# A two-layer decoder on one core: convolution by taps on VectorE, down products on two banks, query transposes behind the scores

## The chip, the cores and the metric

The kernel runs on one core of a Trainium2 chip. A core has a matrix engine (TensorE, called PE in the profile), three engines for elementwise work (VectorE or DVE, ScalarE or ACT, GpSimd or POOL), an engine that mainly issues transfers (SyncE or SP) and 16 DMA engines. Data lie in SBUF (128 partitions) and in PSUM, where TensorE writes its results. Each engine works through its own instructions in order and waits on semaphores for the others. The metric is the device time of one execution in microseconds; lower is better.

## The reference

x has 4 batches of 256 tokens with 256 features, in fp32; a context of 4 x 256 x 128 feeds a state-space branch. In each of two layers three branches are added to x, each on a layernorm of x:

```python
x = x + attn0(layernorm(x))            # 8 heads of 32, window of 64, tanh softcap
x = x + mamba0(ctx, layernorm(x))      # 256 channels, 16 states
x = x + ffn0(layernorm(x))             # ternary SwiGLU, 704 inner features
x = x + attn1(layernorm(x))            # 16 heads of 128, 4 key/value heads, causal
x = x + mamba1(ctx, layernorm(x))
x = x + moe(layernorm(x))              # 32 experts of 128, top 6 by groups, one shared
```

The state-space branch (mamba) is, for each channel e:

```python
xc = inproj @ ctx                       # 256 x 128 by 128 x 256
u  = silu(causal_conv(xc, w[e, 0:4]) + bias)        # 4 taps, each channel alone
dt, B, C = softplus(dtproj @ (xproj @ u)), ...
h[t] = h[t-1] * exp(dt * A) + dt * u * B ; y = sum_n h * C + D * u
out = y * silu(layernorm(x))
```

The dense feed-forward part is `down(silu(gate(x) * gate_s) * up(x) * up_s) * down_s`. The second attention normalises queries and keys over their 128 features, applies gains, biases and a rotation, and then a causal softmax.

## The kernel before, in words

x stays in SBUF as `x` from the first transfer to the last. The text of the kernel goes through the layers in order, but the framework's planner puts the instructions of each engine into an order of its own: it goes by the place of an instruction in the text, by when it reckons the operands to be ready, and by when a buffer of the pools comes free. So a line written earlier may be issued later. The state-space scans are generators of steps (`mamba_scan`, lines 201 to 239) which the text starts among the other work, so that the scan of one layer fills the engines while attention or a feed-forward part goes on.

**State-space front** (`mamba_front`, L150 to L199, called for two halves of the batches in each layer). For each of two blocks of 128 channels (c) it takes one PSUM bank and makes the convolution on TensorE: four matmuls (L166) whose weights `taps` are the input projection times one tap each, with the context shifted by one column per tap. ScalarE applies bias and Silu from the bank to `u` (L173). Then come the x projection (L179), dt (L188, softplus L190), `du` (L193) and y's start (L196). `conv_taps` (L297 to L317) makes the weights for a layer: a diagonal of the taps on VectorE (L304), two matmuls with ones (L311) and two products with the input projection (L312). For layer 1 it is called at L590. All banks of the front come from the pool pf, which has one.

**Scan** (`state`, L212 to L221): exp on ScalarE (L215), dt·u·B on GpSimd (L217), the scan on VectorE (L218) and its product with C (L220); the sum over states is shared by TensorE (L235 with an identity) and GpSimd (L227, L237), and L239 adds what TensorE summed. `mamba_gate` multiplies with the gate (L263), transposes (L265) and adds to x (L271).

**Feed-forward part of layer 0** (L576 to L640). There are two halves hf of 512 tokens. For each of six chunks ic of the inner features: two products of two matmuls (L606), Silu on ScalarE (L614), and the product `hT` on VectorE (L617). Then two pairs of token tiles (t2) take one bank of the pool pa (one buffer) each, 12 matmuls (L630), and L638 adds the bank to x. At the end of each half the front of layer 1 for the same half is called. ScalarE needs a different table for Silu than for the scan's Exp, and loading one shows in the trace as an instruction of its own at L215 or L614.

**Second attention** (L643 on). 16 steps: 4 batches times 4 key/value groups g. `keys_values` makes the layernorm of a batch, transposes it (`ln_transposed`, L140) and makes the keys. `queries` (L710) projects 512 query columns for two token tiles (`rotate`: L673, squares L688, rotation L693, L700, L701 to `qr`), transposes each (`transposed`: four transposes L707 into a bank of ps_t, copy L708 to `qT`), and takes the root (`rsqrt`, L665, L666) to `rq`. `score` makes the scores of a step (L771, L780, L773, L789, the softmax L799 to L804), `finish` transposes the weights (L814, L822), multiplies with the values (L827, L828) and projects out (L842). The steps are staggered: queries of one step, scores of the step ahead, the finish of the one ahead of that:

```python
qT = ap.tile([P, 4, S], F32, tag="qT", name="qT", bufs=2)
rq = queries(xnT, g, qT)
queued.append((b, g, qT, rq, kT, xnT))
if len(queued) > 1:
    score()
if len(scored) > 1:
    finish()
```

The scan of layer 1 runs beside it, 19 of its 32 steps during the first 13 attention steps (`EARLY`), and the rest beside the first half of the MoE part (L974, L979, L988), which ends the kernel. PSUM has 8 banks: in the first part pools pa 1, pb 2, pc 1, psd 2, psy 1, pf 1; in attention ps_q 2, ps_s 1, ps_t 2, ps_o 1 and the scan's 2.

Of the kernel before, what the change touches and what calls it, by code (L numbers as in the profile page):

```python
# [13 lines left out]
AF = mybir.ActivationFunctionType  # L14
# [3 lines left out]
P = 128  # L18
# [23 lines left out]
def decoder_kernel(  # L42
# [107 lines left out]
    def mamba_front(l, bp, pool):  # L150

        taps, xproj, dtproj = mw[l]
        o = l * M_COLS
        u = front.tile([P, 2, 512], F32, tag="u", name="u")
        dt = front.tile([P, 2, 512], F32, tag=f"dt{bp}", name="dt")
        du = front.tile([P, 2, 512], F32, tag=f"du{bp}", name="du")
        y = front.tile([P, 2, 512], F32, tag=f"y{bp}", name="y")
        xdbl = front.tile([40, 512], F32, tag="xdbl", name="xdbl")
        negA = front.tile([P, 32], F32, tag="negA", name="negA", bufs=2)

        bc = dpool.tile([32, 512], F32, name=f"bc{l}{bp}")

        for c in range(2):
            pi = ps(pool)
            for k in range(4):
                mm(  # L166
                    pi.rearrange("p (b t) -> p b t", b=2),
                    lhsT=taps[:, k, c * P : (c + 1) * P],
                    rhs=ctxT[:, 2 * bp : 2 * bp + 2, k : k + S],
                    start=(k == 0),  # L170
                    stop=(k == 3),
                )
            nc.scalar.activation(  # L173
                u[:, c, :], pi, AF.Silu, bias=par[:, o + M_CONVB + c : o + M_CONVB + c + 1]
            )

        px = ps(pool)
        for c in range(2):
            mm(px[0:40, :], lhsT=xproj[:, c, :], rhs=u[:, c, :], start=(c == 0), stop=(c == 1))  # L179
        nc.scalar.copy(xdbl, px[0:40, :])  # L180
        nc.sync.dma_start(out=bc, in_=xdbl[8:40, :])


        nc.scalar.activation(negA, par[:, o + M_ALOG : o + M_ALOG + 32], AF.Exp)
        nc.vector.tensor_scalar(negA, negA, 1e-25, -1.0, ALU.max, ALU.mult)
        for c in range(2):
            pd = ps(pool)
            mm(pd, lhsT=dtproj[:, c * P : (c + 1) * P], rhs=xdbl[0:8, :], start=True, stop=True)  # L188
            z = dt[:, c, :]
            nc.scalar.activation(  # L190
                z, pd, AF.Softplus, bias=par[:, o + M_DTB + c : o + M_DTB + c + 1]
            )
            nc.vector.tensor_mul(du[:, c, :], z, u[:, c, :])  # L193

            nc.gpsimd.memset(z.rearrange("p (s t) -> p s t", s=2)[:, :, 0:1], 1e28)
            nc.scalar.activation(  # L196
                y[:, c, :], u[:, c, :], AF.Copy, scale=par[:, o + M_D + c : o + M_D + c + 1]
            )
        y_of[l, bp] = y  # L199
        return dt, du, y, negA, bc  # L200
# [376 lines left out]
    with ExitStack() as ph:  # L577
# [9 lines left out]
        nc.sync.dma_start(out=dw, in_=down_in)  # L587
        nc.gpsimd.tensor_mul(dw, dw, downs.unsqueeze(1).to_broadcast([P, NIC, HID]))

        conv_taps(1)  # L590
        scans = []
        for hf in range(2):
            szs = [gates_of(2 * hf + bb, fp, 4) for bb in range(2)]
            if hf == 1:
                states(99)
            xnT = wp.tile([P, 2, 512], F32, tag="f_xnT", name="f_xnT")
            for bb in range(2):
                mamba_gate(0, 2 * hf + bb, pc, szs[bb])
                ln_transposed(2 * hf + bb, xnT[:, :, bb * S : (bb + 1) * S], pc)
            hT = wp.tile([P, NIC, 512], F32, tag="hT", name="hT")  # L600
            for ic in range(NIC):
                m = min(P, INTER - ic * P)
                pg, pu = ps(pb), ps(pb)
                for dst, w in ((pg, gw), (pu, uw)):
                    for f in range(2):
                        mm(  # L606
                            dst[0:m, :],
                            lhsT=w[:, f, ic * P : ic * P + m],
                            rhs=xnT[:, f, :],
                            start=(f == 0),  # L610
                            stop=(f == 1),
                        )
                sg = fp.tile([P, 512], F32, tag="sg", name="sg")
                nc.scalar.activation(  # L614
                    sg[0:m, :], pg[0:m, :], AF.Silu, scale=par[0:m, P_GATES + ic : P_GATES + ic + 1]
                )
                nc.vector.scalar_tensor_tensor(  # L617
                    hT[0:m, ic, :],
                    pu[0:m, :],
                    par[0:m, P_UPS + ic : P_UPS + ic + 1],  # L620
                    sg[0:m, :],
                    ALU.mult,
                    ALU.mult,
                )
            for t2 in range(2):
                pd = ps(pa)
                for t in range(2):
                    for ic in range(NIC):
                        m = min(P, INTER - ic * P)
                        mm(  # L630
                            pd[:, t * HID : (t + 1) * HID],
                            lhsT=hT[0:m, ic, (2 * t2 + t) * P : (2 * t2 + t + 1) * P],
                            rhs=dw[0:m, ic, :],
                            start=(ic == 0),
                            stop=(ic == NIC - 1),
                        )
                xb = x[:, 4 * hf + 2 * t2 : 4 * hf + 2 * t2 + 2, :]
                nc.vector.tensor_add(xb, xb, pd.rearrange("p (t d) -> p t d", t=2))  # L638
            scans.append(mamba_front(1, hf, pf))
# [4 lines left out]
    with ExitStack() as ph:  # L644
# [62 lines left out]
                nc.tensor.transpose(pt[:, i * P : (i + 1) * P], qr[:, i, :], ident)  # L707
            nc.scalar.copy(dst[:, :, c * P : (c + 1) * P], pt.rearrange("p (h t) -> p h t", h=4))  # L708

        def queries(xnT, g, qT):  # L710

            ss = small.tile([P, 2, 4], F32, tag="qss", name="qss")
            for c in range(2):
                transposed(rotate(xnT, c, g, ss[:, c, :]), c, qT)
            return rsqrt(ss, qks)

        def keys_values(b):
            xnT = work.tile([P, 2, S], F32, tag="xnT", name="xnT")
# [320 lines left out]
        for b in range(B):  # L1039
            xnT, kT = keys_values(b)  # L1040
            for g in range(NKV1):
                qT = ap.tile([P, 4, S], F32, tag="qT", name="qT", bufs=2)
                rq = queries(xnT, g, qT)
                queued.append((b, g, qT, rq, kT, xnT))
                if len(queued) > 1:
                    score()
                if len(scored) > 1:
                    finish()
                step = 4 * b + g

                with tc.issue_after(pace[-3]) if len(pace) > 2 else nullcontext():
                    if step < 13:
                        run(states, EARLY * (step + 1) // 13 - EARLY * step // 13)
                if step == 12:
                    for bb in range(2):
                        mamba_gate(1, bb, ps_t)

                    spare[:] = [psd, ps_s, psd]
                if step > 12:
                    next(moes[0])  # L1060
# [126 lines left out]
```

## Time and profile before

| what | value |
| --- | --- |
| three runs | 898.40, 910.52, 914.03 us (median 910.52) |
| the profiled execution | 899.79 us, its span 898.0 us |
| mean granted TensorE clock | 0.947 |
| second attention, 310 to 651 us | TensorE 300.7 busy of 341 |
| MoE alone, 760 to 898 us | TensorE 133.3 busy of 138 |
| scan of one state on VectorE, L218 | 1.217 us |
| product with C, L220 | 0.680 us |
| loading a table on ScalarE | 1.28 us |

The profile is of one execution. Its page gives the busy time of each engine, the span in 40 slices, and the chain of work that ended last, followed back from the end; the groups of instructions give the line, the engine, the operation, what is written from what, the count, the busy time, the mean of one in ns, and the idle time just before them with what ended it. The view of stages gives the busy time in chosen stretches. A tile named `ps` is a PSUM bank. An fp32 matmul leaves two records in the trace, a transpose of 128x128 too.

### The profile page before, as it was taken

The page shows a single profiled execution, that of the slowest core. Times are in us where ns is not written, and L with a number is a line of the kernel's source. Part 1 is how long each engine was busy: PE and PEld are TensorE (multiplying, and loading weights), DVE is VectorE, ACT ScalarE, POOL GpSimd, SP SyncE. Part 2 cuts the span into 40 slices and gives each one's busy share as a digit, 9 for nine tenths or more (in the row PEclk, how much of TensorE's full clock was granted, in tenths as well). Part 3 has the DMA queues.
Part 4 walks back from the last instruction along what each step waited for, and adds up shares of the span by engine and source line. Part 5 has one row for each costly group of instructions (what it writes and reads, how often), then busy time and mean ns, then how long its engine had stood idle before and what let it go on. Part 6 is the DMA issues. An engine that isn't in the chain of part 4 may idle for free.

```text
span 898.0 us, 10284 instructions
## 1 busy us (share of the span) xinstructions
PE 806.3 (90%) x3074; PEld 501.4 (56%) x3074; DVE 588.0 (65%) x1106; ACT 474.5 (53%) x1182; POOL 423.5 (47%) x427
## 2 busy tenths in 40 slices
PE   4888999978989887889788978997999999999997
PEld 1445656523444444647555755665666656666665
DVE  4799988985855588797769686787057676212121
ACT  2767544587949556657857754776333433211111
POOL 5456676976645527766547471422257751000000
PEclk9999767978998999999899989997999999999999
DMA  5347564583512401101112010000147753445442
GB/s 162 117 133 252 174 187 157 186 275 100 198 64 68 143 1 36 59 33 39 36 36 72 23 47 1 24 3 24 27 152 226 231 152 104 148 149 162 156 144 82
DMA packets 60999, 98.36 MB, mean 110 GB/s; under 512 B 6336, under 2 KB 26704, under 8 KB 60688
## 3 DMA queue, kind: packets, MB, share of 16 engines
q1 hardware_dynamic: 59232, 95.77, 33.6%
q10 hardware_dynamic: 1712, 1.94, 0.7%
q8 instruction: 24, 0.39, 0.2%
q14 instruction: 31, 0.25, 0.1%
HBM read 96.24 MB, written 1.44 MB: 109 GB/s over the span
## 4 chain that ended last, share of the span: by engine, by line
PE 51%; DVE 20%; ACT 10%; issue 5%; POOL 4%; DMA 1%; DVEq 0%; POOLq 0%; SPq 0%; ACTq 0%
PE ps L974 13%; PE ps L988 12%; PE ps L842 5%; DVE h L218 4%; PE ps L673 3%; DVE hc L220 2%; PE ps L606 2%; PE ps L630 2%; PE ps L827 2%; DVE ps L700 2%; ACT sc L799 2%; DVE qs L693 2%; PE ps L780 1%; ACT L215 1%; PE ps L235 1%
## 5 line engine op out<-in xcount | busy, mean ns | idle before, releaser
L217 POOL TENSOR_TENSOR db<-bt,du 128x512 f32<-128x512 f32 x128 | 162.4, 1280 | 90.7 <-DVE h L218 76.3
L218 DVE TENSOR_TENSOR_SCAN h<-h,db 128x512 f32<-128x512 f32 x128 | 152.9, 1217 | 25.9 <-ACT h L215 25.7
L974 PE MATMUL ps<-moe_xnT,w 128*128 128x512 f32 x272 | 129.0, 597 | 0.0
L988 PE MATMUL ps<-w,hT 128*128 128x256 f32 x544 | 128.7, 380 | 0.0
L979 DVE SCALAR_TENSOR_TENSOR hT<-ps,gr 128x512 f32<-128x512 f32 x64 | 44.1, 689 | 127.0 <-PE ps L974 127.0
L988 PEld LDWEIGHTS ps<-w,hT 128*128 128x128 f32 x544 | 103.2, 191 | 40.2 <-issue 29.4
L215 ACT ACTIVATE h<-dt,negA 128x512 f32<-128x512 f32 x128 | 86.2, 689 | 56.3 <-DVE hc L220 55.7
L980 ACT ACTIVATE hT<-hT 128x512 f32<-128x512 f32 x68 | 42.8, 629 | 133.8 <-DVE hT L979 133.6
L673 PE MATMUL ps<-wqkv,xnT 128*128 128x512 f32 x192 | 93.2, 597 | 8.0 <-DVE rq L665 5.6
L220 DVE TENSOR_TENSOR hc<-h,ct 128x512 f32<-128x512 f32 x128 | 85.1, 680 | 4.0 <-DMA ct<-bc 2.5
L227 POOL TENSOR_TENSOR y<-y,hc 128x512 f32<-128x512 f32 x64 | 80.8, 1274 | 7.1 <-DVE hc L220 7.1
L666 POOL TENSOR_TENSOR rq<-rq,nhalf 128x8 f32<-128x8 f32 x20 | 33.0, 1648 | 88.2 <-DVE rq L665 88.0
L974 PEld LDWEIGHTS ps<-moe_xnT,w 128*128 128x128 f32 x272 | 51.7, 191 | 36.5 <-issue 33.2
L688 ACT ACTIVATE sq<-ps 128x128 f32<-128x128 f32 x160 | 42.4, 282 | 46.2 <-PE ps L673 46.2
L799 ACT ACTIVATE sc<-sc,nm 128x256 f32<-128x256 f32 (+1 forms) x128 | 56.7, 449 | 12.2 <-DVE nm L794 8.0
L804 POOL TENSOR_TENSOR sc<-sc,rsum 128x512 f32<-128x512 f32 (+1 forms) x32 | 46.3, 1468 | 35.2 <-DVE rsum L802 33.6
L842 PE MATMUL ps<-wo,oT 128*128 128x256 f32 x256 | 57.0, 381 | 0.4 <-ACT oT L835 0.4
L842 PEld LDWEIGHTS ps<-wo,oT 128*128 128x128 f32 x256 | 48.1, 190 | 9.2 <-ACT oT L835 2.6
L673 PEld LDWEIGHTS ps<-wqkv,xnT 128*128 128x128 f32 x192 | 32.9, 190 | 29.1 <-issue 17.9
L235 PE MATMUL ps<-hc,ident 128*128 128x512 f32 x64 | 40.6, 723 | 8.1 <-DVE hc L220 8.1
L707 PE MATMUL ps<-ident,qr 128*128 128x128 f32 x160 | 28.7, 297 | 19.2 <-DVE qr L701 17.3
L237 POOL TENSOR_TENSOR y<-y,hc 128x512 f32<-128x512 f32 x32 | 40.8, 1275 | 10.4 <-DVE hc L220 5.3
(201 smaller groups left out, 1447.3 us busy)
## 6 DMA issues: line engine op xcount, KB each, us to landing
bt<-bc SPq DMA_DIRECT2D x96, 256.0 KB, 3.6
ct<-bc SPq DMA_DIRECT2D x96, 256.0 KB, 3.7
w<-in_w_dram SPq DMA_DIRECT2D x64, 256.0 KB, 3.4
gr<-gt SPq DMA_DIRECT2D x64, 256.0 KB, 3.5
wqkv<-in_wqkv_dram SPq DMA_DIRECT2D x1, 3072.0 KB, 14.4
wo<-in_wo_dram SPq DMA_DIRECT2D x1, 2048.0 KB, 8.9
x<-in_x_dram SPq DMA_DIRECT2D x4, 256.0 KB, 5.6
w<-in_ws_dram SPq DMA_DIRECT2D x4, 256.0 KB, 3.4
```

The source lines that it names most:

```text
L215: nc.scalar.activation(h, dt[:, c, :], AF.Exp, scale=negA[:, a : a + 1])
L217: nc.gpsimd.tensor_mul(db, bt, du[:, c, :])
L218: nc.vector.tensor_tensor_scan(h, h, db, 0.0, ALU.mult, ALU.add)
L220: nc.vector.tensor_mul(hc, h, ct)
L227: nc.gpsimd.tensor_add(y[:, c, :], y[:, c, :], state(n, c, bt, ct))
L235: mm(yp, lhsT=ident, rhs=hc, start=(n == 0), stop=(n == 14))
L673: mm(pq, lhsT=xnT[:, f, c * P : (c + 1) * P], rhs=wqkv1[:, f, ch * 512 : (ch + 1) * 512], start=(f == 0), stop=(f == 1),)
L799: nc.scalar.activation(part, part, AF.Exp, bias=nm[:, qc, j : j + 1], accum_out=rsum[:, qc, j : j + 1])
L804: nc.gpsimd.tensor_mul(part, part, rsum[:, qc, :].unsqueeze(2).to_broadcast([P, 4, w]))
L842: mm(pout[:, c * 256 : (c + 1) * 256], lhsT=oTs[h // 4][:, h % 4, c * P : (c + 1) * P], rhs=wo1[:, 8 * gp + h, :], start=(h == 0), stop=(h ...
L974: mm(ph_, lhsT=w[:, f * P : (f + 1) * P], rhs=xnT[:, f, :], start=(f == 0), stop=(f == 1))
L988: mm(po[t // 2][:, (t % 2) * 256 : (t % 2 + 1) * 256], lhsT=h[:, t * P : (t + 1) * P], rhs=w[:, 256:512], start=start and t % 2 == 0, stop ...
```

## The change

Three parts. In `mamba_front` for layer 1 the convolution is one matmul with the unscaled input projection per block of channels, and then four instructions on VectorE that read the bank: one product with the last tap (written to `u`), and three fused multiply-adds on 255, 254 and 253 of each batch's 256 columns, shifted by one, two and three. ScalarE then applies bias and Silu in place on `u`. The call of `conv_taps` for layer 1 goes. In the feed-forward part the two pairs of token tiles take their banks from the pools pa and pc in turn. In the second attention `queries` returns the rotated queries, and their transposes come in the text after the scores of the step ahead, which no longer wait for the new step to be queued. Layer 0 keeps its convolution on TensorE.

```diff
@@ mamba_front
         for c in range(2):
             pi = ps(pool)
+            if l == 1:
+
+                mm(
+                    pi.rearrange("p (b t) -> p b t", b=2),
+                    lhsT=taps[:, c * P : (c + 1) * P],
+                    rhs=ctxT[:, 2 * bp : 2 * bp + 2, 3 : S + 3],
+                    start=True,
+                    stop=True,
+                )
+                w = par[:, o + M_CONVW + 4 * c : o + M_CONVW + 4 * c + 4]
+                uc = u[:, c, :].rearrange("p (b t) -> p b t", b=2)
+                pt = pi.rearrange("p (b t) -> p b t", b=2)
+                nc.vector.tensor_scalar(uc, pt, w[:, 3:4], None, ALU.mult)
+                for k in range(1, 4):
+                    nc.vector.scalar_tensor_tensor(
+                        uc[:, :, k:S], pt[:, :, 0 : S - k], w[:, 3 - k : 4 - k], uc[:, :, k:S], ALU.mult, ALU.add
+                    )
+                nc.scalar.activation(
+                    u[:, c, :], u[:, c, :], AF.Silu, bias=par[:, o + M_CONVB + c : o + M_CONVB + c + 1]
+                )
+                continue
             for k in range(4):
                 mm(
@@ feed-forward part of layer 0
-        conv_taps(1)
         scans = []
...
             for t2 in range(2):
-                pd = ps(pa)
+                pd = ps((pa, pc)[t2])
@@ second attention
-        def queries(xnT, g, qT):
+        def queries(xnT, g):
 
             ss = small.tile([P, 2, 4], F32, tag="qss", name="qss")
-            for c in range(2):
-                transposed(rotate(xnT, c, g, ss[:, c, :]), c, qT)
-            return rsqrt(ss, qks)
+            qrs = [rotate(xnT, c, g, ss[:, c, :]) for c in range(2)]
+            return qrs, rsqrt(ss, qks)
...
             for g in range(NKV1):
+                qrs, rq = queries(xnT, g)
+                if queued:
+                    score()
                 qT = ap.tile([P, 4, S], F32, tag="qT", name="qT", bufs=2)
-                rq = queries(xnT, g, qT)
+                for c in range(2):
+                    transposed(qrs[c], c, qT)
                 queued.append((b, g, qT, rq, kT, xnT))
-                if len(queued) > 1:
-                    score()
                 if len(scored) > 1:
                     finish()
```

## The prediction

> **What bounds the kernel now.** I read the busy table first, then the chain, then a table of stages.
>
> Page, parts 1 and 4:
>
> ```profile
> PE 806.3 (90%) x3074; PEld 501.4 (56%) x3074; DVE 588.0 (65%) x1106; ACT 474.5 (53%) x1182; POOL 423.5 (47%) x427
> ...
> PE 51%; DVE 20%; ACT 10%; issue 5%; POOL 4%; DMA 1%; DVEq 0%; POOLq 0%; SPq 0%; ACTq 0%
> ```
>
> TensorE is busy 90% of the span, but only 51% of the chain is TensorE: there are stretches where something else ends last. The stage table tells which (columns: PE, PEld, DVE, ACT, POOL busy us with instruction counts, granted clock, DMA share, GB/s):
>
> ```profile
> 150.00:213.00 63.00, 52.92 (x194) 27.92 (x190) 51.31 (x83) 40.87 (x67) 47.53 (x51) 0.85 0.61 197
> 213.00:250.00 37.00, 35.89 (x90) 16.57 (x91) 27.17 (x34) 32.49 (x39) 25.95 (x25) 0.95 0.51 171
> 250.00:270.00 20.00, 15.70 (x53) 7.64 (x51) 9.78 (x29) 9.45 (x14) 7.71 (x16) 0.95 0.18 58
> 270.00:310.00 40.00, 36.44 (x102) 18.11 (x102) 21.62 (x30) 30.35 (x35) 22.71 (x26) 0.94 0.37 118
> 310.00:651.00 341.00, 300.74 (x1265) 199.39 (x1266) 251.60 (x524) 215.89 (x770) 166.31 (x140) 0.96 0.09 30
> 651.00:760.00 109.00, 106.59 (x381) 69.76 (x380) 72.83 (x146) 39.86 (x63) 59.94 (x57) 0.98 0.55 171
> ```
>
> The rows are: end of the layer-0 scan; FFN half 0; the passage between halves; FFN half 1; second attention; MoE beside the last scan. The change works in the first five. TensorE idles 10 us in the first, 1 in half 0, 4 in the passage, 4 in half 1 and 40 in attention; VectorE idles 12, 10, 10, 18 and 89. From 651 on TensorE has 2 us to spare in 109, and its order there is the same in the changed program: that stage keeps its length.
>
> **The change part by part.** Durations are of the profiled execution: span 898.0 us, device time 899.79. The order of instructions per engine is read from the built program, which has no times. Two records make one fp32 matmul.
>
> *Convolution by taps.* TensorE drops 16 matmuls L166 for 4, and the two matmuls L311 that made the weights. On average an L166 record is 630 ns busy, but records overlap: two 512-column records in a row take 0.86 us (L166 on the chain at 229.14). So 12 x 0.86 = 10.3 and 2 x 0.86 = 1.7: 12 us less on TensorE. VectorE drops the diagonal (L304, 1.6 at most) and two L312 of 0.68 (2.9 in all) and gains 16 taps. No tap is in the trace; the nearest rows, both reading a PSUM bank of 128x512, are
>
> ```profile
> L617 DVE SCALAR_TENSOR_TENSOR hT<-ps,par,sg 128x512 f32<-128x512 f32 (+1 forms) x6 | 4.5, 743 | 0.0
> L979 DVE SCALAR_TENSOR_TENSOR hT<-ps,gr 128x512 f32<-128x512 f32 x64 | 44.1, 689 | 127.0 <-PE ps L974 127.0
> ```
>
> I take 0.69, the row with 64 samples: 11.0 us, so +8 net on VectorE (bounds per tap 0.60, as back-to-back spacing shows elsewhere, to 0.75: +7 to +9). The Silu (0.69, L173) stays, one table load fewer among them.
>
> What lies on the path, in three places. (1) Before half 0 (150–213): TensorE stands on the chain at 203.95 with L166 for 1.81, and ACT with L173's table loads at 178.70 and 183.83, 1.28 each. The order puts 8 taps here (5.5) for 2.9 removed: +2.6 on VectorE, whose 12 us of idle time is nearly all waits on the scan's exponentials (10.0 us, L218 waiting for L215); that idle time is the cover. I take −1.8 and one table load, −1.2: **−3**. If the idle time lies at other moments than the taps, the 2.6 shows and the −1.2 is lost: ends −7 (all of TensorE's relief counts) and +3.
>
> (2) Half 0 and the passage. The other 8 taps come between the first four hT products; 10 us of VectorE idle time covers 5.5. But they push scan work back: five scan states stand behind the last hT instead of three, 2 x (1.22 for L218 + 0.68 for L220) = +3.8. The end of that scan is what half 1 needs (y, gate L263, transposes L265, x, layernorm). Against it, L166 and the wait for u leave the passage: TensorE waited 1.52 for u at 260.59, −1.5, and −0.8 is left over from the earlier L166 pairs. **+1.5**, ends −4 (the whole L166/L179 stretch, 256.3 to 263.2, leaves the path) and +5.5 (all eight taps show).
>
> *Down products on two banks*, half 1:
>
> ```profile
> 298.30 3.68 PE L630 MATMUL ps<-dw,hT 64*128 64x256 f32 x14 [0.45 <-DVE hT L617]
> 303.74 6.03 PE L630 MATMUL ps<-dw,hT 128*128 128x256 f32 x24 [1.76 <-DVE x L638]
> 310.60 1.95 PE L673 MATMUL ps<-wqkv,xnT 128*128 128x512 f32 x4 [0.83 <-issue]
> ```
>
> The second pair of token tiles waits until L638 has emptied the one bank: 1.76 us idle, and all its 24 records lie behind the last hT. With two banks both pairs run along with the hT products, and 28 records are left behind the last: 28 x 0.253 (6.03/24 and 3.68/14) = 7.1 instead of 3.68 + 1.76 + 6.03 = 11.5: −4.4. Bringing forward the others makes TensorE 3.43 + 0.86 = 4.29 us per chunk where ACT's alternation of Silu and Exp (sg at 280.76, 284.77, 288.77, 292.77) has 4.0: +0.3 for each of four, +1.2; the last two chunks run without an Exp between, one table load pair of 2.56 less, of which I count 0.6. The bank that is borrowed, pc, also serves the layernorm transposes of the first attention batch: these ran inside half 1 (275.96) and now wait for the second L638 (0.69), then copy, then L673: +1.4 beyond the 0.8 gap shown. If that cover stays, 0. Half 0 has no such wait at the moment, its four L235 fill the gap. Sum −4.4 + 1.2 − 0.6 + 1.4 = −2.4; I add −1.2, since TensorE idles 4 us in this row and the earlier matmuls fill part of it: **−3.6**, ends −6 and 0.
>
> *Query transposes behind the scores.* The waits of TensorE in 310–651 (instruction, releaser, us, times, longest):
>
> ```profile
> PE ps L707 <- DVE qr L701: 17.3, 9, 4.7
> PE ps L673 <- DVE rq L665: 5.6, 4, 1.8
> PE ps L780 <- DVE sc L773: 2.6, 3, 1.3
> PE ps L814 <- POOL sc L804: 2.1, 2, 1.5
> PE ps L737 <- ACT kT L708: 1.9, 2, 0.9
> ```
>
> 17.3 us of waiting for rotated queries is the obvious prize, and four waits make 14.3 of it (2.94 at 357.67, 3.21 at 438.90, 3.43 at 523.13, 4.72 at 611.30). But the order in which the program is issued is the planner's, not the text's: around three of the four, in batches 0, 2 and 3, L707 already stands right behind the score matmuls L771 and still does. At 438.90 all eight transposes now stand together behind L771, and more scan steps (1.9 each) get in front of the rotation on VectorE. Elsewhere scores do pass the transposes: the five short waits, 3.0 us in all, have work in front of them now. What is late next is the query itself: qT ready later, its scores at the next step later, but there a whole step (21 us) lies between. No instruction is added; SP's and POOL's orders are the same. I take **−2** (ends −17, every qr wait gone, and +6, one of the four places doubled plus a wait of 1.3 for sc in each following batch).
>
> Sum: −3 + 1.5 − 3.6 − 2 = **−7.1**: 892.7 on the profiled execution's footing.
>
> A rule that speaks against taking work from TensorE: rows first. In 150–213 the granted clock was 0.85, TensorE was busy 84%, and one pair of L235 took 2.08 us at 198.83 against 1.11 at 224.16. The Trainium skill ("TensorE: Matmul & The Clock Gate", Part 1: The HAM clock gate) says that the clock falls to half after an idle window of some 3.4 us and returns after as long a busy one. By it, thinning TensorE by 10 us in this stage could make several matmuls like that L235, at 1 us each, eating place (1)'s gain. No run here shows it yet.
>
> **Rivals.**
> A. *The qr waits go.* For it: it is the largest wait of the stage, and a transposes-last order gives the chain sq, qs, ps, qr (1.15 + 0.69 + 0.70 + 0.69 = 3.2 us) eight score matmuls to hide behind. Against it: the order at three of four places. −14 to −17 in place of −2: about −20, 880 on the profile's footing, 890 on the median's.
> B. *The change does not do what it says*: the planner holds the waits where they were, and the taps push the scans as far as TensorE is relieved: stage one 0, passage +3.8, half 1 −3.6, attention 0: 0 ± 3, 900 to 910.
> C. *Slower: the taps stand in the scan.* The pool pf has one bank. It used to be free after matmul and Silu; now it is held until the fourth tap, and taps stand among scans on an in-order VectorE. If two scan states get between the taps of each c, that is 4 x 0.69 + 2 x 1.9 = 6.6 us a bank, and TensorE waits at the next matmul on pf with everything behind it. Price: two banks before half 0, one effective, +6.6; passage +5.5; half 1 −3.6; attention 0: +8.5, 908 to 919. It decides once VectorE's idle time in 150–270 (32 us) does not lie where the taps stand. For it: VectorE is 81% busy in the first stage. Against: taps are placed among hT products that it did without idle.
>
> **How the numbers follow.** The executions shown lie at 898.4, 899.8 (profiled), 910.5 and 914.0, and 2% (18 us) is about what a measurement of this kernel can tell from no change. The profiled one is 10.7 below the median of the runs, so −7.1 gives 892.7 on its footing and 903.4 on the median's; I name 900, nearer the latter. Forecast 0.50, A 0.17, B 0.20, C 0.13. The low end is A on the profile's footing with its end of −19: 881; the high end C on the median's: 919. What passes 2% faster is A, with a little of the forecast; slower, a third of C: 0.18, 0.77, 0.05.
>
> **What would show it.** TensorE busy about 12 us lower; L166 replaced by 8 records; 16 taps near 0.69; no idle time for L638 in front of L630; hT6 to the first L673 about 4 us shorter; MoE's stretch equally long. L707 waiting for qr: 14 or more says forecast, under 5 says A. VectorE idle in 150–270 under 20 with half 1 starting 5 later says C. I am wrong if the taps take over 0.9, or if attention gets a new wait as long as those it lost.

## The result

The changed kernel takes 918.40 us (median of 4 runs, 912.06 to 921.70); the kernel before took 906.38 us beside it (median of 4, 898.40 to 914.03). The ratio is 1.0138 with an interval of 1.0091 to 1.0186: 1.4% **slower**, 12 us. The forecast was 900, six below the kernel before as measured here. The time lies in the range of 881 to 919, on the wrong side of the kernel before.

The profiled execution of the changed kernel took 912.06 us, its span 910.2. Page, part 1, busy time of each engine:

```profile
PE 797.5 (88%) x3046; PEld 497.3 (55%) x3046; DVE 598.9 (66%) x1119; ACT 471.8 (52%) x1180; POOL 421.8 (46%) x427
```

TensorE is 8.8 us less busy (806.3 before) and VectorE 10.9 more (588.0), while the span is 12.2 longer. The work moved the way that was forecast (12 less and 8 more); the time went the other way. The table of stages, with the same columns as before:

```profile
150.00:213.00 63.00, 41.02 (x166) 23.09 (x165) 52.96 (x85) 37.75 (x63) 45.91 (x47) 0.79 0.63 200
213.00:250.00 37.00, 35.38 (x86) 15.83 (x86) 26.80 (x34) 33.23 (x38) 20.76 (x23) 0.91 0.36 117
250.00:270.00 20.00, 14.89 (x47) 7.24 (x46) 15.47 (x26) 10.66 (x14) 11.93 (x12) 0.96 0.50 157
310.00:651.00 341.00, 299.55 (x1249) 196.57 (x1248) 256.77 (x530) 211.39 (x764) 167.63 (x144) 0.96 0.11 36
```

In the first row, whose length is fixed, TensorE has 11.9 us less work (52.9 to 41.0); the granted clock is 0.79, where it was 0.85. That its work was not what this stretch waited for shows in the next table: the way to half 0 became longer, not shorter.

To see where the 12 us arose, I mark six instructions that both kernels have: the second of the four additions of layer-0 attention to x (on VectorE), the addition of the first gate, the first L606 of half 0, the last addition to y of the layer-0 scan (L239), the first L606 of half 1, the first L673 of the second attention, and the end. Lines are those of the kernel before; the changed kernel's lie 19 to 21 higher.

| stretch, us | before | after | difference | forecast |
| --- | --- | --- | --- | --- |
| up to the second addition to x | 134.4 | 135.1 | +0.6 | 0 |
| to the first gate's addition | 60.3 | 58.3 | −2.0 | |
| to half 0 | 19.0 | 24.0 | +5.0 | −3 with the line above |
| half 0 to half 1 | 56.5 | 64.5 | +8.0 | +1.5 |
| (of that, to the scan's end) | 39.5 | 47.4 | +7.9 | |
| half 1 to the second attention | 40.3 | 37.1 | −3.2 | −3.6 |
| second attention to the end | 587.4 | 591.2 | +3.8 | −2 |

Two of the terms held: half 1, and the MoE part, whose stretch from the last output projection of attention to the end is 246.9 us before and 245.9 after. The 12 us arise in three places: the stretch that ends at the start of half 0, the one up to the end of the layer-0 scan, and attention.

### The profile page after: what moved, and what is told of

It is laid out like the page before. It is cut to its first block, busy times and chain, and to the rows that moved or that the text cites. A ratio compares the mean times of both kernels' runs of the same rounds, so it can differ in the third digit from the quotient of the medians.

```text
span 910.2 us, 10230 instructions
## 1 busy us (share of the span) xinstructions
PE 797.5 (88%) x3046; PEld 497.3 (55%) x3046; DVE 598.9 (66%) x1119; ACT 471.8 (52%) x1180; POOL 421.8 (46%) x427
## 4 chain that ended last, share of the span: by engine, by line
PE 41%; DVE 14%; ACT 6%; issue 2%; POOL 2%; DVEq 0%; ACTq 0%; POOLq 0%
PE ps L993 12%; PE ps L1007 12%; PE ps L861 5%; PE ps L693 3%; ACT sc L818 3%; DVE h L239 3%; PE ps L799 2%; PE ps L846 1%; DVE qs L713 1%; DVE sc L808 1%; DVE ps L720 1%; ACT sq L708 1%; PE ps L727 1%; DVE qr L721 1%; DVE nm L814 1%
## 5 line engine op out<-in xcount | busy, mean ns | idle before, releaser
L239 DVE TENSOR_TENSOR_SCAN h<-h,db 128x512 f32<-128x512 f32 x128 | 152.6, 1215 | 7.9 <-ACT h L236 6.5
L693 PE MATMUL ps<-wqkv,xnT 128*128 128x512 f32 x192 | 96.2, 614 | 7.7 <-DVE rq L685 2.5
L818 ACT ACTIVATE sc<-sc,nm 128x256 f32<-128x256 f32 (+1 forms) x128 | 56.6, 445 | 16.1 <-DVE nm L813 9.9
L693 PEld LDWEIGHTS ps<-wqkv,xnT 128*128 128x128 f32 x192 | 33.4, 195 | 29.8 <-issue 18.4
L727 PE MATMUL ps<-ident,qr 128*128 128x128 f32 x160 | 28.9, 302 | 17.6 <-DVE qr L721 13.8
```

The costliest lines, as they stand in the source:

```text
L239: nc.vector.tensor_tensor_scan(h, h, db, 0.0, ALU.mult, ALU.add)
L693: mm(pq, lhsT=xnT[:, f, c * P : (c + 1) * P], rhs=wqkv1[:, f, ch * 512 : (ch + 1) * 512], start=(f == 0), stop=(f == 1),)
L818: nc.scalar.activation(part, part, AF.Exp, bias=nm[:, qc, j : j + 1], accum_out=rsum[:, qc, j : j + 1])
```

## The experiments

One thing has to be known to read them. The first 134 us differ between executions of one and the same program: two of the kernels below (two banks; second bank only in half 0) have the instructions of the kernel before up to half 0. The second addition to x comes at 134.4 us in the kernel before and at 144.8 and 145.2 in these, with a granted clock from 75 to 100 us of 0.90, 0.69 and 0.70. So executions of one kernel spread over 12 to 15 us (the kernel before, in its three longer series), and I read the experiments twice: by the ratio over all runs, and by the lengths of the stretches after that point, which are steadier (the stretch from the first gate to half 0 is 18.9 to 19.1 in all six executions that share its program; the whole way from the second addition to half 0 is 79.3 to 81.2). Each stretch is that of one profiled execution.

**The three parts one at a time, and two together.**

The convolution alone:

```diff
 # kernel before
+            if l == 1:
+                (one matmul, four taps on VectorE, Silu in place)
-        conv_taps(1)
```

> The kernel before with the convolution by taps alone. Theory T (the taps cost the time): the loss before FFN half 1 is the convolution's, so half 0 starts 3 to 4 us later than before and half 1 a further 6 to 8 later; in all 9 to 14 us slower than the kernel before, as much as or more than the whole change. Rival R (the borrowed bank costs it, by changing the order at the end of half 0): 0 to 4 slower. Rival S (each part is harmless, together they collide): within 3 us of the kernel before.

Measured: 922.95 us, ratio 1.021 (1.0179 to 1.0242). Half 0 starts 86.2 us after the second addition (79.3 before), half 0 to half 1 takes 62.5 (+6.0), half 1 39.7. Theory T is right on the place of the loss; its size passed the range. All of its four executions lay within 0.7 us and at a low granted clock (0.914 to 0.915; the kernel before in the same series 0.932 to 0.948), and the profiled one had lost 8 us before the second addition; counted from there it is 14.5 us longer than the kernel before.

Two banks alone:

```diff
-                pd = ps(pa)
+                pd = ps((pa, pc)[t2])
```

> The kernel before with the down products on two banks alone. Theory T: the wait of 1.76 us in half 1 goes, half 1 is 3 us shorter, the passage between the halves is as long as before: 2 to 4 us faster. Rival R: the passage grows by 4 to 8 us, 2 to 6 us slower in all. Rival S: 2 to 4 faster.

Measured: 909.08 us, ratio 1.0059 (1.0023 to 1.0096). Theory T falls here: half 1 became 2.7 us shorter (37.6), but half 0 to half 1 became 6.3 us longer (62.8). Rival R is right.

The moved transposes alone (`queries` returns the rotated queries, `score()` comes ahead of `transposed`, as in the change):

> The kernel before with the query transposes behind the scores alone. Theory T: three of the four long waits keep their place, so attention (310 to 651 us before) changes by less than 3 us either way. Rival Q (the 3.8 us that the first attention batch lost come from this part): 2 to 5 us slower, and the loss lies in the first batch. The forecast's own case A (the waits go): 14 us faster.

Measured: 910.87 us, ratio 1.0042 (1.0002 to 1.0083). From the second attention to the end 589.8 us, 2.4 longer. The waits did not go. From the first L673 to the last output projection attention takes 343.9 us for 340.5, a little past theory T's 3. Rival Q is wrong on the place: up to the end of the first output projection 2.4 us are lost, but kernels without this part lose 1.7 to 3.0 there too. Where it does cost, the section on attention below shows.

Banks and transposes, without the convolution:

> The changed kernel with the convolution undone. Theory T: FFN as in the kernel with two banks, attention as in the kernel with moved transposes: 1 to 5 us faster than the kernel before, 10 to 16 faster than the changed kernel. Rival R: slower than before by 2 to 6. Rival S: 2 to 6 faster than before.

Measured: 908.13 us, ratio 1.0029 (0.9983 to 1.0076); half 0 to half 1 62.9, half 1 37.6, attention to the end 588.0. Theory T's 1 to 5 us faster than the kernel before did not come, since it still counted on the banks. As with the banks alone, the stretch before half 1 is 6.3 longer. So two parts lose in the same stretch, each about 6 us alone and 8 together: their losses overlap.

**Which half the second bank costs in.** It was given to one half only:

```diff
-                pd = ps(pa)
+                pd = ps((pa, pc)[t2 * hf])          # only half 1
+                pd = ps((pa, pc)[t2 * (1 - hf)])    # only half 0, the other kernel
```

> The kernel before, with the second bank only in FFN half 1; half 0 keeps one bank. Theory K: in half 0 the second bank lets 28 down-product records stand in one row on TensorE ahead of the last state sums (L235), which delays the end of the layer-0 scan by 6 to 7 us; in half 1 no sum stands behind and 2.7 us are won. So the passage is as before, half 1 2 to 3.5 us shorter: 1 to 4 us faster than the kernel before. Rival W (the waits of the scan's own buffers cost it, wherever the bank is): same as with two banks in both halves, 2 to 6 slower.

> The kernel before, with the second bank only in FFN half 0. Theory K: the stretch from the start of half 0 to the start of half 1 is 5 to 7 us longer (62 to 63), half 1 as before (40): 4 to 8 us slower than the kernel before. Rival W (the two halves only cost together): within 2 us.

Measured, only half 1: **902.82 us, ratio 0.9945 (0.9904 to 0.9986)**, faster than the kernel before; half 0 to half 1 57.5, half 1 37.5 (−2.8). Only half 0: 909.55, ratio 1.0027 (0.9985 to 1.0069); half 0 to half 1 62.8 (+6.3), half 1 40.1. Theory K's stretches are right in both; the total of the second was forecast as 4 to 8 slower, and its interval ends at 6. In the profiled execution with the bank in half 1 only 0.4 us of the gain are left from the second addition to the end, since 1.0 is lost ahead of half 1 and 1.4 behind it: that this kernel is faster rests on the ratio, whose interval ends just under 1.

Why half 0 loses shows in TensorE's timeline. The kernel before, end of half 0 (start, length, instruction, count of records, idle time before):

```profile
244.76 3.68 PE L630 MATMUL ps<-dw,hT 64*128 64x256 f32 x14 [0.26 <-DVE hT L617]
248.37 1.98 PE L235 MATMUL ps<-hc,ident 128*128 128x512 f32 x4
250.19 5.93 PE L630 MATMUL ps<-dw,hT 128*128 128x256 f32 x24
256.05 0.44 PE L265 MATMUL ps<-ident,yg 128*128 128x128 f32 x2
```

The same place with two banks alone:

```profile
257.83 1.02 PE L235 MATMUL ps<-hc,ident 128*128 128x512 f32 x2
258.78 7.09 PE L630 MATMUL ps<-dw,hT 64*128 64x256 f32 x28
265.80 3.90 PE L235 MATMUL ps<-hc,ident 128*128 128x512 f32 x8
269.53 0.38 PE L265 MATMUL ps<-ident,yg 128*128 128x128 f32 x2
```

Before, the second group of products could not start until L638 had emptied the bank, and the last sums over scan states (L235) got in between. With the second bank nothing holds the products back: 28 records stand in one row, and the sums behind them. The scan waits for these sums, because each frees a buffer `hc` and the last one frees y. The wait that the change removed was the gap in which the work ran on which half 1 depends.

To test this reading, the rest of the layer-0 scan was written ahead of the down products, with two banks, with one, and in the whole changed kernel:

```diff
-            if hf == 1:
-                states(99)
...
+            if hf == 0:
+                states(99)
             for t2 in range(2):
```

> The kernel before with two banks in both halves, and the rest of the layer-0 scan written ahead of the down products of half 0, not behind them; on TensorE all state sums now stand ahead of the last 40 records of the down products. Theory K (the row of 28 ahead of the sums is what cost 6 us): the scan's end comes at 40 us after the start of half 0 or earlier (46.4 with two banks), the stretch from half 0 to half 1 falls from 62.8 to 58 or less. Rival W (the sums' place does not matter, the second bank costs through the order on VectorE and GpSimd): it stays above 61.

> The kernel before with the same move of the scan's rest alone, one bank. Theory K: the sums already stood ahead of the second group before, so the move gains little: the stretch from half 0 to half 1 is 54 to 58 (56.5 before). Rival W: as much gain as with two banks, some 5 us.

> The whole changed kernel with the scan's rest written ahead of the down products of half 0. Theory K with T: the stretch from half 0 to half 1 falls from 64.5 to 57 to 60, the taps' share in it stays; the stretch before half 0 stays 2 to 6 longer than before: 4 to 7 us faster than the changed kernel, 5 to 8 slower than the kernel before. Rival (the taps' delay is the same delay and goes too): as fast as the kernel before.

With two banks the row now stands behind the sums:

```profile
247.88 1.13 PE L235 MATMUL ps<-hc,ident 128*128 128x512 f32 x2
248.85 0.59 PE L630 MATMUL ps<-dw,hT 128*128 128x256 f32 x2
249.69 1.12 PE L235 MATMUL ps<-hc,ident 128*128 128x512 f32 x2 [0.25 <-DVE hc L220]
250.66 10.17 PE L630 MATMUL ps<-dw,hT 128*128 128x256 f32 x40
```

The scan ends 34.0 us after the start of half 0 (46.4 with two banks), and half 0 to half 1 takes 54.6 us in place of 62.8. Rival W falls; with one bank the same move leaves this stretch at 57.6. But the times are 908.77, ratio 1.0033 (0.9981 to 1.0086), and 903.81, ratio 0.9999 (0.9943 to 1.0055): from the second attention to the end the first takes 601.0 us, 13.6 longer than the kernel before. The move changed half 1 as well: the products there no longer run along with the hT products, and the layer-1 fronts stand later. GpSimd is 186.0 us busy in the first 340 us of attention, where it was 166.3:

```profile
311.05:651.05 340.00, 291.45 (x1214) 192.20 (x1213) 266.13 (x538) 220.76 (x777) 186.01 (x156) 0.95 0.14 44
```

The kernel before, same length from its own first L673:

```profile
310.60:650.60 340.00, 300.33 (x1263) 199.01 (x1264) 251.03 (x523) 215.89 (x770) 166.31 (x140) 0.96 0.09 30
```

So layer-1 scan work that had run inside the feed-forward part now runs in attention, and what the shorter FFN won is given back there. In the whole changed kernel the move gives 912.33 us, ratio 1.0071 (1.0031 to 1.0112): half 0 to half 1 56.6, so the taps' share of that stretch goes with the row's; the stretch before half 0 stays long (24.3 from the first gate), and attention to the end takes 597.8, 6.6 more than in the changed kernel.

**Where the taps cost.** One front at a time, with the weights for the other one made as before:

```diff
+            if l == 1 and bp == 0:     # the front ahead of half 0; the other kernel: bp == 1
+                (taps on VectorE, lhsT=inproj1)
+        inproj1 = mw[1][0]
         conv_taps(1)
```

> The kernel before, with the convolution by taps only for the first front of layer 1, the one that runs ahead of FFN half 0; the weights for the second front are made as before. Theory T: the taps stand between the layernorm of the first batch and the start of half 0 on VectorE: 4 to 6 us slower from the first gate's addition to half 0; the rest as before. In all 3 to 7 us slower. Rival U (only the second front's taps cost): within 2 us.

> The kernel before, with the convolution by taps only for the second front, whose taps stand among the hT products of half 0. Theory T: 8 taps of 0.69 us push the scan's states back, its end comes 5 to 7 us later after the start of half 0, half 1 starts as much later: 4 to 8 us slower. Rival U: the whole loss of the convolution, 12 to 17.

Measured: first front 907.25, ratio 1.0016 (0.9971 to 1.0061); second front 910.14, ratio 1.0025 (0.9989 to 1.0060). Both expectations on the mechanism missed. With the first front's taps the stretch ahead of half 0 did not grow (16.8 from the first gate, 79.0 from the second addition); half 0 to half 1 grew by 3.4, since scan states slid into half 0. With the second front's, half 0 to half 1 took 63.1 (+6.6, as long as forecast), but the scan's end was nearly on time (40.4 after the start of half 0, 39.5 before): the delay arose behind it. By the ratios the two cost 4 us together, far below the 17 of the convolution alone; counted from the second addition in the profiled executions they are 2.5 and 7.1 us longer than the kernel before, the convolution alone 14.5.

What these two had in common was that the making of the tap weights stayed in the program. It was left in for both fronts, with nothing reading the weights:

```diff
+            if l == 1:
+                (taps on VectorE, lhsT=inproj1)
+        inproj1 = mw[1][0]
         conv_taps(1)
```

> The convolution by taps for both fronts alone, with the making of the tap weights of layer 1 (the diagonal, two matmuls and two products) left in the program, though nothing reads them. The convolution alone cost 17 us, its two fronts one at a time, which keep this work, some 1 and 4. Theory G (leaving out this early work moves the phase in which the clock is granted in layer-0 attention): the granted clock between 75 and 100 us is back at 0.85 or more, 3 to 9 us slower than before. Rival H (the two fronts together simply cost more): 14 or more slower.

Measured: 908.99 us, ratio 1.0028 (0.9987 to 1.0070). Rival H falls: with 3 us of VectorE and two matmuls more to do, it is 14 us faster than the kernel without them. Of the difference, 7.2 us lie between the second addition and half 0 (79.0 against 86.2) and 6.5 ahead of it. Not all of the loss is gone: half 0 to half 1 takes 64.8 in it, 8.3 more than in the kernel before, and from the second addition to the end its profiled execution is 7.5 us longer. The clock from 75 to 100 us was 0.86 in its profile and 0.66 in that of the convolution alone, as theory G has it. But that this is caused by the missing work was not shown: the changed kernel and the one with the bank in half 1 only (below) have the same program as the convolution alone up to half 0, and had 0.88 and 0.86 there (the second lost 8.6 us ahead of the second addition all the same, with a clock of 0.50 from 120 to 140 us). One program draws either. The part in the stretch before half 0 is another matter: it is the order, and the next experiment takes it up.

In the changed kernel, VectorE ahead of half 0:

```profile
195.15 0.40 DVE L120 BATCH_NORM_STATS2 ln_st<-x 128x6 f32<-128x256 f32 x1
...
196.46 3.03 DVE L284 TENSOR_TENSOR yg<-y,sz 128x256 f32<-128x256 f32 x1
199.41 0.17 DVE L121 BATCH_NORM_AGGREGATE ln_mv<-ln_st 128x2 f32<-128x6 f32 x1
```

GpSimd at the same time:

```profile
195.79 3.42 POOL L609 TENSOR_TENSOR dw<-dw,downs 128x1536 f32<-128x1536 f32 x1 [4.17 <-DMA dw<-in_down_dram]
199.16 1.45 POOL L258 TENSOR_TENSOR y<-y,hc 128x512 f32<-128x512 f32 x1
200.69 0.22 POOL L124 TENSOR_SCALAR ln_nb<-ln_mv 128x2 f32<-128x2 f32 x1
```

And TensorE:

```profile
204.06 1.18 PE L140 MATMUL ps<-ident,xn 128*128 128x128 f32 x4 [10.68 <-ACT xn L136]
```

A gate product that has a median of 0.42 us over its 16 instructions takes 3.03, and ends 0.3 us after GpSimd's multiplication of the down weights; the layernorm's last step stands behind it, then GpSimd's part of the layernorm, and TensorE waits 10.68 us. In the kernel before the multiplication ran from 200.57 to 204.00, behind GpSimd's part of this layernorm (197.02 to 198.60) and where VectorE was waiting for L190 anyway. In the changed kernel the transfer of dw is issued 3.1 us earlier (187.1 for 190.2) and the multiplication starts 4.8 earlier. That alone does not make the collision: with the weights' work kept, the multiplication starts 1.5 us after the first gate's addition (2.4 in the changed kernel), but the gate product stands right behind that addition, ahead of the multiplication, and takes 1.18. In the changed kernel a scan state, its product with C and a part of the layernorm stand between. With the multiplication cut into six:

```diff
-        nc.gpsimd.tensor_mul(dw, dw, downs.unsqueeze(1).to_broadcast([P, NIC, HID]))
+        for ic in range(NIC):
+            nc.gpsimd.tensor_mul(dw[:, ic, :], dw[:, ic, :], downs)
```

> The changed kernel, with GpSimd's one multiplication of the down weights (3.42 us, 128x1536) cut into six of a sixth each. In the changed kernel it runs while VectorE wants to do a gate product of 0.4 us, which takes 3.03 us there, and the layernorm of the first batch waits behind it. Theory L (the two engines exclude each other for the whole instruction): the gate product takes 1.2 us at most, the stretch from the first gate's addition to half 0 falls from 24.0 by 2 to 3 us, in all 2 to 4 us faster than the changed kernel, 8 to 11 slower than the kernel before. Rival O (the order of the taps alone makes this stretch): it stays at 24, in all 12 slower than before.

Measured: 914.55 us, ratio 1.0092 (1.0047 to 1.0138); the gate product takes 1.43, a little over the 1.2 expected, and the first gate to half 0 takes 21.4 in place of 24.0 to 25.7 in the executions with one multiplication. Theory L is right for the stretch. That leaves 2.4 us over the 19.0 before, whose cause was not tested: in the changed kernel the two dt products of the first front (L209) stand right ahead of half 0 and wait 1.20 and 1.56 us, where before (L188) they were done by 202.9. And counted from the second addition, the way to half 0 is 83.1 here and 81.1 to 86.2 with one multiplication, so the gain shows only behind the first gate. Its profiled execution, 926.59 us, is its longest (half 0 to half 1 69.3), so its later stretches are not read; the totals' intervals overlap, and the gain of 4 us against the changed kernel is not shown by them.

Last, two kernels that move or remove a part. The convolution by taps alone, with each front held back until the last addition of its FFN half:

```diff
+                last = nc.vector.tensor_add(xb, xb, pd.rearrange("p (t d) -> p t d", t=2)).ins
+            with tc.issue_after(last):
+                scans.append(mamba_front(1, hf, pf))
```

> The convolution by taps alone, each front of layer 1 held until the last addition of its own FFN half has been issued, so that no tap stands ahead of the layer-0 scan. The first scan states of layer 1 lose their place in half 1 with it and move into attention. Theory T (place of the taps, not their amount): half 0 starts as early as in the kernel before or earlier, the scan's end no later: 0 to 8 us faster than the kernel before. Rival V (11 us of VectorE work cost what they cost wherever they stand, and the scan states moved into attention lengthen it): 8 or more slower than before.

Measured: 940.14 us, ratio 1.0316 (1.0217 to 1.0414). No tap stood ahead of half 0 now, and yet half 0 started 84.0 us after the second addition, 4.7 later than in the kernel before. The scan's end came early (35.8 after the start of half 0), but half 0 to half 1 took 61.2, since the taps now stood in the passage, and attention to the end 608.6, 21 us more. Rival V is right, through the scan states that moved.

The changed kernel with the second bank only in half 1:

> The changed kernel, with the second bank only in FFN half 1. Theory K with T: the delay by the row of 28 and that by the taps lie on the same scan's end and overlap; without the row the stretch from half 0 to half 1 falls from 64.5 to 61 to 63, half 1 stays at 37 to 38: 2 to 4 us faster than the changed kernel, 8 to 11 slower than before. Rival (they add up): 58 to 59 and 6 us faster than the changed kernel.

Measured: 916.15 us, ratio 1.0094 (1.0052 to 1.0137); half 0 to half 1 63.3, half 1 37.0. The row's and the taps' delays overlap: taking one away in the presence of the other wins 1.2 us in the stretch, where alone it was worth 6.

## Why the prediction was wrong, step by step

**What bounds the kernel.** The reading "TensorE idles 10 us in the first, 1 in half 0, 4 in the passage" was right as a count and wrong in its use. I valued TensorE's relief there as time; the stretches up to half 1 end with a chain through VectorE, GpSimd and ScalarE, on which a shorter TensorE only waits longer (10.68 us at the first L140 ahead of half 0).

**(1) Before half 0**, forecast −3, measured +3.0 (−2.0 and +5.0). The failed step is "I take −1.8 and one table load, −1.2": neither was won. Two readings under it were wrong: of VectorE's 12 us of waiting only 2.1 are L218 waiting for L215 (9.6 more lie in half 0), and the diagonal ran at 18.3 us, so that of the 2.9 removed only the two L312, 1.4, leave this stretch. Still, it was not the cover that failed: with the weights' work kept, the second addition to half 0 takes 79.0 us with the first front's taps, 79.0 with both (79.3 before), and 84.0 without that work and with no tap there. What I counted as won, leaving out the weights' work, changed the order. Not on the list was GpSimd's dw product, 3.42 us, which now stood ahead of the layernorm of the first batch and blocked a gate product; it is 2.6 of the 5.0 by the split kernel, and the rest stays open.

**(2) Half 0 and the passage**, forecast +1.5, measured +8.0. I counted five scan states behind the last hT in place of three, as the trace has it, and priced them at +3.8, but put them down to the taps alone. The convolution alone brings 6.0, the banks alone 6.3, which I had at nothing. The sentence that failed is "Half 0 has no such wait at the moment, its four L235 fill the gap": the gap was how L235 came in time. The −1.5 for the wait for u and −0.8 for L166 were no gain either: from the scan's end to half 1 it takes 17.0 us before and 17.1 after. That passage is a chain (gate, transposes, x, layernorm, transposes, for one batch and then the other), and what TensorE dropped beside it did not shorten it.

**(3) Half 1**, forecast −3.6, measured −3.2. The 28 records behind the last hT took 7.09 us in the kernel with the bank in half 1 (7.1 forecast). From the last product to the first L673 the changed kernel needs 2.65 us, 1.8 more than before (+1.4 forecast):

```profile
308.25 8.15 PE L650 MATMUL ps<-dw,hT 128*128 128x256 f32 x32
317.18 0.44 PE L679 MATMUL ps<-ident,bt 128*128 128x128 f32 x2 [0.78 <-DVE x L658]
317.45 0.60 PE L140 MATMUL ps<-ident,xn 128*128 128x128 f32 x4
319.05 5.40 PE L693 MATMUL ps<-wqkv,xnT 128*128 128x512 f32 x8 [1.00 <-ACT xnT L143]
```

**(4) Attention**, forecast −2, measured +3.8. TensorE's waits from 310 to 665 us of the changed kernel (instruction, releaser, us, times, longest):

```profile
PE ps L727 <- DVE qr L721: 13.8, 8, 4.7
PE ps L799 <- DVE sc L792: 3.1, 3, 1.7
PE ps L727 <- DVE qr L745: 2.7, 3, 1.8
PE ps L693 <- DVE rq L685: 2.5, 2, 1.3
PE ps L846 <- ACT pTa L844: 2.4, 4, 1.0
PE ps L790 <- DVE e L765: 2.4, 2, 1.2
```

Most of the long waits stayed, as forecast (13.8 of 17.3, a hair under the 14 that I had named as the sign), so rival A fell for the reason given, the order. I had the wrong ones, though: 3.14, 3.94 and 4.71 us are left, and gone is the 3.43 of batch 2 (523.13), one of those that were to stay. The 3.5 us won came back as waits for the offsets, the keys and the weights; the waits of this view add up to 39 us before and 41 after. I had also not counted that after a wait TensorE may run at half its clock. The kernel before, at the first of its long waits (a transpose leaves one record, L707 160 for its 160 transposes, and not two, as it says ahead of the prediction):

```profile
357.67 0.66 PE L707 MATMUL ps<-ident,qr 128*128 128x128 f32 x4 [2.94 <-DVE qr L701]
358.79 1.13 PE L780 MATMUL ps<-kT,qT 128*128 128x256 f32 x4 [0.46 <-DVE sc L773]
```

The changed kernel, same place:

```profile
367.78 1.11 PE L727 MATMUL ps<-ident,qr 128*128 128x128 f32 x4 [3.14 <-DVE qr L721]
369.75 2.08 PE L799 MATMUL ps<-kT,qT 128*128 128x256 f32 x4 [0.86 <-DVE sc L792]
```

The same matmuls take 1.7 and 1.8 times as long, and the granted clock of the next 7 us is 0.53 (1.00 before). But the 0.2 us more of waiting do not decide it. The kernel with two banks alone waited exactly as long as the kernel before, and its clock fell at once:

```profile
374.89 1.12 PE L707 MATMUL ps<-ident,qr 128*128 128x128 f32 x4 [2.94 <-DVE qr L701]
```

With the bank in half 1 only, the clock stayed up after the same 2.94 us; both kernels take 66.7 us to the end of the first output projection. The kernel before, too, lost its clock after its waits of 3.21 and 4.72 us, and over the whole of attention the granted clock is 0.96 in both. So the clock at this one wait is not what attention lost.

Up to the end of its first output projection attention lost 3.9 us; kernels of this study that have other parts of the change, but not the moved transposes, lost 1.7 to 3.0 there, so most of it is not the work of the transposes. 1.7 of it is the opening, where the eight L693 took 5.40 us for 3.67: the granted clock of the first 7 us is 0.76 there, as in four other kernels with the second bank in half 1, and 1.00 before. The rest is open.

One stretch is the transposes' own: between two output projections, from batch 2 to batch 3, it takes 47.1 us in all six kernels with moved transposes and 44.5 in all eleven without. TensorE waits 1.8 us there for the keys (L727 for L745), which it did not before, and the granted clock is 0.96, where it was 1.00. Other steps make up for part of that.

**Rivals.** C, the slower one, came closest: +8.5 for 12, with +5.5 in the passage and −3.6 in half 1. But its mechanism, TensorE blocked at the bank of pf, did not occur: no wait of TensorE for a tap appears in its waits up to 310 us, and VectorE's idle time from 150 to 270 us is 24.8 us, not under the 20 named as its sign. When the weights' work stays, the taps give +2.5 by the ratio, inside B's 0 ± 3, but +7.5 from the second addition on, with 8.3 ahead of half 1 where B had 3.8. The taps themselves were sized right: 16 for 11.6 us, 0.73 each (0.69 forecast).

**The clock rule.** The Trainium skill ("TensorE: Matmul & The Clock Gate", Part 1: The HAM clock gate) gives half the clock after an idle window of some 3.4 us. The traces agree that a wait can halve the clock, but not in the length: 2.94 us halved it in the kernel with two banks and left it in the kernel before, and 3.14 halved it in the changed one. The 10.68 before half 0 went with a granted clock of 0.79 for 0.85. I had weighed the rule for stage (1) and left it out of the sum, and did not ask it of attention at all.

## What to carry to other kernels

Before taking a wait away, ask who works in it: here the wait for a bank was the gap through which the sums reached TensorE that the next phase depended on, and taking it away where nothing stood behind (half 1) won 0.55% (0.14 to 0.96) while the same edit in half 0 lost 6 us of its stretch. Time of a busy engine is worth something only in a stretch whose end it sets; relieve it elsewhere and its idle time grows. And where a planner orders the work, an edit of one part moves others: leaving out some early work let a GpSimd instruction that ran 5 us earlier meet VectorE's path, and work held out of the feed-forward part came back in attention.

## What the runs showed of the hardware

A VectorE product with both inputs in SBUF and a GpSimd product exclude each other for a whole instruction: one of 128x256, 0.42 us by the median, took 3.03 to 3.35 us in four executions in which it met GpSimd's 3.42 us multiplication, and 1.43 when that was cut in six. The product with C, one of whose inputs lies in PSUM, keeps its length: 0.69 us in the kernel before at 223.40, while GpSimd's product (1.28 us from 223.39) runs. The Trainium skill ("SBUF — State Buffer", Who interferes with whom) says so: a VectorE product with both inputs in SBUF and a GpSimd instruction that reads SBUF share a port pair, and the second to issue is blocked until the first has finished. The traces agree.

The granted clock of the same instructions in layer-0 attention, between its first and its second addition to x, came out at 0.65 to 0.78 in the six executions that share the program up to half 0, and the second addition at 133.3 to 145.2 us. What decides it is open. Nor does the length of a wait alone decide whether the clock falls behind it: after 2.94 us at the same place in attention it stayed up for 7 us in two kernels and fell at once in two others.
